# Masked graph attention on one core: the stores of h on ScalarE's queue, the stores of u on SyncE's, and an eleventh warming matmul

## The chip, the cores and the metric

The kernel runs on one core of a Trainium2 chip. Its engines are TensorE (PE in the profile, PEld for its weight loads), VectorE (DVE), ScalarE (ACT), GpSimd (POOL) and SyncE (SP), which only issues DMAs. ScalarE and GpSimd can issue DMAs too. The metric is the device time of one execution in microseconds; a time for a kernel is the median of its runs.

## The reference

A layer of attention over a sparse graph with 2708 nodes and 1024 features, after a layer norm, with a residual:

```python
h = jnp.maximum(_layernorm(x, axis=-1), 0.0)
q = h @ W_q.T + b_q;  k = h @ W_k.T + b_k;  v = h @ W_v.T + b_v
z = (q @ k.T) / sqrt(1024)
z = z * adj                                   # adj: 0 or 1, about 4 ones in a row
z = jnp.where(z == 0.0, -10000.0, z)
out = x + relu(softmax(z, axis=1) @ v)
```

## The kernel before

The kernel never forms the 2708 x 2708 scores. It finds the few neighbours of each node in the adjacency, sorts the nodes by their number of neighbours, and works on 22 row tiles of 128 nodes (the last has 20). Three streams run beside each other.

The matmul stream is TensorE's. After `WARM` matmuls on zeros (lines 497 and 498), which depend on nothing but a cleared tile, it forms M from W_q and W_k in a fast scheme of blocks (line 463: `term`, in PSUM banks ps_x, ps_y, ps_z; ScalarE takes the results out in `evicted`, line 477, VectorE in `joined`). Then come 20 units, each two row tiles against one matrix of 1024 x 1024 in a block scheme of seven products (`multiply`, line 982, matmuls at line 948). Ten units are "q" (rows of h times M) and ten are "o" (rows of u times W_v); one tile is left alone at the end. Before a unit its rows are transposed (`half_turned`, line 402, tiles pt) and copied out by ScalarE (`held`, line 684). ScalarE also sets the starting value of two banks (`banks_for`, line 713), copies a bank to psy and to p5 (lines 961 and 964), and copies results.

The preparing stream loads x (line 218) and the adjacency (line 347) on SP, forms h in place on ScalarE (`apply`, line 263), counts ones on ScalarE (`counted`, line 355) and finds their places on VectorE (line 376). The factors r of the layer norm come from GpSimd (`root`, lines 246 to 254). Each tile of h is written to DRAM (`keep`, line 270) and summed into `hsum` on GpSimd (lines 272 and 285). A tile's buffer is used again for a later tile of x, and that load waits for both the store and the sum. The table of neighbours is scattered to DRAM in sorted order by GpSimd (`put`, line 613) in two parts, late tiles first, and read back (`reload`, line 625); the part of tiles 0 to 7 is the early table.

The attention stream gathers rows of h by the table on GpSimd (line 597), forms scores on VectorE (line 826) against q, which SP loads (line 799), and weighted sums u on VectorE (line 879), whose first term is ScalarE's (line 871). Ten of the u tiles are written to `u_dram` (`sums`, line 888) and read back by SP as rows of an "o" unit (line 1142, tiles or); the other tiles stay in SBUF. SP also stores q (line 1022), stores combinations of W_v in `tv_dram` (line 768) and reloads M and T for the "o" units (line 1247).

The order on ScalarE and VectorE is the order of the code through the first four units, and on VectorE through all of the units; GpSimd's is written by hand up to the table's reload. The string `steps_at` and the calls of `follow` place single steps (h and k are `keep`, a is `apply`, p is `counted`, r is `root`) between the products. A planner orders the rest, SP among it. Each engine works through its own instructions strictly in that order.

Of the kernel before, what the change touches and what calls it, by code (L numbers as in the profile page):

```python
# [18 lines left out]
P = 128  # L19
# [10 lines left out]
EARLY = 8  # L30
# [4 lines left out]
WIDE = 8  # L35
MOMENTS = (0, 1, 2, 3, 6, 7)
ROOT = 32
WARM = 10
SEARCH = tuple(range(EARLY, 22)) + tuple(range(EARLY))
BATCHES = ((0, 3), (4, 7), (8, 11), (12, 12), (13, 13), (14, 17), (18, 21))  # L40
MLIMIT = 61.0 / 512
# [22 lines left out]
def tile_preln_masked_attention(  # L64
# [12 lines left out]
    nc = tc.nc  # L77
# [23 lines left out]
    h_dram = dram.tile([N, D], FT, name="h_dram")  # L101
    q_dram = dram.tile([EARLY * P, D], FT, name="q_dram")
    q_late = dram.tile([(BARE - EARLY) * P, D], FT, name="q_late")
    u_dram = dram.tile([FULL * P, D], FT, name="u_dram")
# [30 lines left out]
    ptab = tab  # L135
# [30 lines left out]
    t = 0  # L166
    while t < NT:
# [4 lines left out]
        t = e  # L172
# [92 lines left out]
    def keep(first, add=True):  # L265

        group, xs, r = normed.pop(first)
        for t, xt in zip(group, xs):
            t0, n = tiles[t]
            (nc.scalar if 6 <= t <= 10 else nc.gpsimd).dma_start(h_dram[t0:t0 + n, :], xt[:n])  # L270
            if add:
                nc.gpsimd.tensor_add(hsum[:n], hsum[:n], xt[:n])
            else:
                owed[t] = xt
# [21 lines left out]
    def follow(steps):  # L296

        for step in steps.split():
# [11 lines left out]
            elif step[0] in "hk":  # L310
                keep(first, step[0] == "h")
            elif step[0] == "+":
                owe(first)
            elif step[0] == "p":
                counted(first)
            elif step[0] == "c":
                counts(*halves[first])
            elif step[0] == "o":
                sorted_at.append(sort(*halves[first]))
            elif step[0] == "w":  # L320
                pooled.close()
                with tc.issue_after((behind if first < EARLY else products)[-1].ins):
                    entered.append(put(first, int(last[0]) + 1))
            elif step == "z":
                pooled.enter_context(tc.manual_schedule(engines={mybir.EngineType.Pool}))
                with tc.issue_after(entered[-1].ins):
                    reload(EARLY, NT)
            elif step[0] == "b":
                reload(*halves[first])
            elif step[0] == "g":  # L330
                squared(first)
            else:
                if step[0] == "e":
                    counted(first)
                if step[0] != "j":
                    found(first, *[range(int(o[0]), int(o[-1]) + 1) for o in only])
                if step[0] != "i":
                    listed(first)
# [94 lines left out]
    with tc.tile_pool(name="w", bufs=1, side="left") as wp:  # L433
# [62 lines left out]
        zeros = hsum.bitcast(BF)  # L496
        for i in range(WARM):
            cleared = nc.tensor.matmul(Y[i % H], zeros[:, :P], zeros[:, :NB], start=True, stop=True)  # L498
# [122 lines left out]
    def reload(lo, hi):  # L621

        full = min(hi, FULL)
        src = tab_dram[lo >= EARLY]
        loads = [nc.gpsimd.dma_start(ptab[:, lo:full, :], src[:(full - lo) * P, :].rearrange("(t p) w -> p t w", p=P))]
        if hi > FULL:
            loads.append(nc.gpsimd.dma_start(ptab[:REST, FULL, :], src[(FULL - lo) * P:, :]))
        for load in loads:
            for put in puts[lo >= EARLY]:
                tc.add_manual_dep(load.ins, put.ins.name,  # L630
                                  mybir.DependencyInfo(mybir.DependencyClass.Sync, mybir.DependencyReason.DATA),
                                  reason="every row of the part")
        return loads[-1]
# [171 lines left out]
    def fill():  # L805
        while wanted and free:
            t, s = wanted.pop(0)
            g = free.pop(0)
            with tc.issue_after(first_q[0].ins) if first_q else nullcontext():
                gathered.append(gather(g, h_dram[:, :], t, s, P, skip=True))  # L810
            g_of[t].append(g)

    def chained(step):

        with tc.issue_after(chain[-1].ins):
            chain.append(step())
# [58 lines left out]
    def sums(t):  # L875
        u, coef = us.pop(t)
        for s in range(0 if t in EMPTY else 1, K[t]):
            fill()
            chained(lambda: nc.vector.scalar_tensor_tensor(  # L879
                u, g_of[t][s], coef[:, at[t][s]:at[t][s] + 1], u, op0=ALU.mult, op1=ALU.add))  # L880
            free.append(g_of[t][s])
            yield 1.3
        fill()
        g_of.pop(t)
        if near(t):
            held[t] = u
        else:
            nc.gpsimd.dma_start(u_dram[t * P:(t + 1) * P, :], u)
        done.add(t)

    def marked(lo, hi):
# [5 lines left out]
    def attention(order):  # L897
        for t in order[:2]:
            ask(t)

        fetch(order[0])
        fill()
        yield 0.0
        marked(0, EARLY)
        free.extend(slots[:8])
        fill()
        yield 0.0
        after = order[1:] + [None, None]
        yield from scores(order[0], after[0])
        for i, t in enumerate(order):  # L910
            nxt = after[i]
            ahead = nxt is not None and K[t] + K[nxt] <= HIGH + 1
            part = scores(nxt, after[i + 1]) if nxt is not None else iter(())
            if ahead:

                for _ in range(min(2, K[nxt] - 1)):
                    yield next(part, 0.0)
            weights(t)
            yield 0.6
            if ahead:  # L920
                yield from part
            yield from sums(t)
            yield from part
# [9 lines left out]
    def near(t):  # L933

        return t == alone or any(t in unit[1:] for unit in units[:now[0] + 3] if unit[0] == "o")
# [72 lines left out]
    lo, hi = slice(0, NB), slice(NB, D)  # L1008
# [295 lines left out]
    with tc.If(some > 0):  # L1304
# [19 lines left out]
        with tc.tile_pool(name="big", bufs=1, side="right") as big, tc.tile_pool(  # L1324
# [34 lines left out]
            with tc.For_i(0, NT) as i:  # L1359
# [35 lines left out]
                for b0 in range(0, N, NB):  # L1395
                    w = min(NB, N - b0)
# [23 lines left out]
                u = gen.tile([P, D + 1], FT, tag="q", name="g_uu")  # L1420
# [60 lines left out]
```

## Time and profile before

| | |
|---|---|
| time, median of 3 runs | 646.41 us (645.72, 646.41, 652.27) |
| profiled execution, its own time | 645.97 us |
| span from first to last instruction | 644.2 us |
| mean granted TensorE clock | 0.997 |
| busy PE / DVE / ACT / POOL | 635.7 / 524.4 / 279.8 / 399.2 us |
| DMA queues, share of 16 engines | POOL's 46.7%, SP's 35.0%, ScalarE's 2.4% |

In the views an engine's name with a q (ACTq, SPq) is its sequencer, which issues DMAs and waits. A row of a timeline has the start and the length in us, engine, line, operation, output<-input and, in brackets, how long the engine sat idle before it and what ended that. A row of a group by source line has the shortest, median and longest duration in ns, and the first and last start in us.

### The profile page before, as it was taken

To read this page: it belongs to the slowest core of one execution; us is meant where nothing else is said; L and a number is where in the kernel's file an instruction comes from. 1 tells how busy PE (TensorE), PEld (TensorE's weight loads), DVE (VectorE), ACT (ScalarE), POOL (GpSimd) and SP (SyncE) were. 2 spreads that over 40 slices of the span, in tenths; PEclk is the share of its full clock that TensorE was granted. 3 is DMA by queue.
4 is the path that set the end of the run, shared out by engine and by line. 5 is a ranking of instruction groups with operands and counts; after the bars stand their busy time and mean duration, and the time that the engine had idled before them with its cause. 6 is when DMAs were issued, how large, how long until landed. Compare 5 with 4: busy or idle time off the path is not lost.

```text
span 644.2 us, 6376 instructions
## 1 busy us (share of the span) xinstructions
PE 635.7 (99%) x1730; PEld 326.2 (51%) x1730; DVE 524.4 (81%) x1014; ACT 279.8 (43%) x426; POOL 399.2 (62%) x428
## 2 busy tenths in 40 slices
PE   9999999999999999999999999999999999999995
PEld 5777766444444444545444444444444544444442
DVE  5999599998896755998988969987999999988121
ACT  3539877958586622413223134332433434423200
POOL 2649991885868457765845536655785868781431
PEclk9999999999999999999999999999999999999998
DMA  8993999599789969997978999988798989895741
GB/s 342 407 362 139 385 342 387 214 323 359 239 313 355 381 206 397 348 356 259 332 248 294 419 415 311 285 269 258 231 338 270 285 303 324 252 285 122 174 135 70
DMA packets 61012, 189.02 MB, mean 293 GB/s; under 512 B 9711, under 2 KB 10047, under 8 KB 60074
## 3 DMA queue, kind: packets, MB, share of 16 engines
q0 software_dynamic: 31728, 98.74, 46.7%
q1 hardware_dynamic: 27514, 84.04, 35.0%
q10 hardware_dynamic: 1728, 5.77, 2.4%
q8 instruction: 16, 0.26, 0.2%
q14 instruction: 26, 0.21, 0.1%
HBM read 159.81 MB, written 42.31 MB: 314 GB/s over the span
## 4 chain that ended last, share of the span: by engine, by line
PE 98%; ACT 0%; POOL 0%; DVE 0%; POOLq 0%; issue 0%
PE ps L948 45%; PE psy L948 32%; PE ps_y L463 6%; PE pt L402 5%; PE ps_x L463 4%; PE ps_z L463 4%; PE ps_y L498 1%; PE ps_h L1153 0%; PE ps_v L581 0%; ACT a L684 0%; DVE y_alone L1297 0%; POOL out_dram L1281 0%; ACT M L477 0%; POOLq L1303 0%; ACT ps L713 0%
## 5 line engine op out<-in xcount | busy, mean ns | idle before, releaser
L597 POOL DMA_INDIRECT g<-h_dram,tab x105 | 127.5, 1214 | 61.3 <-issue 23.5
L948 PE MATMUL ps<-M,a 128*128 128x512 f32 x320 | 144.0, 593 | 0.1
L948 PE MATMUL psy<-wlow,s 128*128 128x512 f32 x320 | 143.9, 592 | 0.0
L826 DVE SCALAR_TENSOR_TENSOR junk<-g,pq 128x1024 uint8<-128x1024 f32 x93 | 113.8, 1223 | 8.1 <-DMA g<-h_dram,tab 6.3
L879 DVE SCALAR_TENSOR_TENSOR u<-g,coef,u 128x1024 f32<-128x1024 f32 x79 | 101.3, 1283 | 5.6 <-ACT u L871 3.7
L948 PEld LDWEIGHTS ps<-M,a 128*128 128x128 f32 x320 | 59.4, 190 | 68.2 <-issue 67.7
L948 PEld LDWEIGHTS psy<-wlow,s 128*128 128x128 f32 x320 | 59.2, 190 | 67.0 <-issue 66.2
L376 DVE FIND_INDEX8 at<-ones,adj 128x8 uint32<-128x685 f32 (+1 forms) x88 | 74.5, 865 | 0.0
L948 PE MATMUL psy<-wlow,a 128*128 128x512 f32 x160 | 72.2, 592 | 0.0
L948 PE MATMUL ps<-wlow,s 128*128 128x512 f32 x160 | 72.0, 593 | 0.0
L948 PE MATMUL ps<-M,s 128*128 128x512 f32 x160 | 71.9, 592 | 0.0
L355 ACT ACTIVATE sized<-adj 128x2708 uint8<-128x2708 f32 (+1 forms) x22 | 54.3, 2468 | 14.2 <-DMA adj<-in_adj_dram 13.4
L1047 POOL DMA_INDIRECT y<-in_x_dram,tab x19 | 34.1, 1793 | 30.6 <-DMA tail_dram<-y 12.5
L285 POOL TENSOR_TENSOR hsum<-hsum,x 128x256 f32<-128x256 f32 (+1 forms) x56 | 38.7, 729 | 22.3 <-DVE wlow L431 15.6
L948 PEld LDWEIGHTS ps<-wlow,s 128*128 128x128 f32 x160 | 30.3, 190 | 38.5 <-issue 36.8
L948 PEld LDWEIGHTS psy<-wlow,a 128*128 128x128 f32 x160 | 30.3, 190 | 37.8 <-issue 37.3
L948 PEld LDWEIGHTS ps<-M,s 128*128 128x128 f32 x160 | 30.3, 190 | 37.8 <-issue 37.3
L778 POOL DMA_INDIRECT out_dram<-y,tab x21 | 29.2, 1392 | 17.3 <-DMA y<-in_x_dram,tab 9.9
L684 ACT COPY a<-pt 128x512 f32<-128x512 f32 x60 | 33.3, 589 | 2.4 <-PE psy L948 2.4
L597 POOL DMA_INDIRECT M<-h_dram,tab x20 | 25.7, 1287 | 13.1 <-ACT u L871 4.6
L688 DVE TENSOR_TENSOR s<-a,pt 128x512 f32<-128x512 f32 x40 | 25.6, 680 | 6.7 <-ACT a L684 5.5
L871 ACT ACTIVATE u<-g,coef 128x1024 f32<-128x1024 f32 x16 | 18.4, 1149 | 25.9 <-DVE coef L870 21.0
(240 smaller groups left out, 867.8 us busy)
## 6 DMA issues: line engine op xcount, KB each, us to landing
adj<-in_adj_dram SPq DMA_DIRECT2D x21, 1354.0 KB
x<-in_x_dram SPq DMA_DIRECT2D x21, 512.0 KB
h_dram<-x POOLq DMA_DIRECT2D x16, 512.0 KB
q_late<-q SPq DMA_DIRECT2D x12, 512.0 KB
pq<-q_late SPq DMA_DIRECT2D x12, 512.0 KB
u_dram<-u POOLq DMA_DIRECT2D x10, 512.0 KB
or<-u_dram SPq DMA_DIRECT2D x10, 512.0 KB
g<-in_wv_dram SPq DMA_DIRECT2D x16, 256.0 KB
```

Of the source, the lines that this page charges most:

```text
L285: small.append(nc.gpsimd.tensor_add(hsum[:n, cols], hsum[:n, cols], xt[:n, cols]))
L355: nc.scalar.activation(sized[:n], a[:n, :, :PW], AF.Abs, accum_out=total[:n, t:t + 1])
L376: nc.vector.max_index(at[:n, k - first_k, g, :], ones[:n, 0:8], a[:n, g, :])
L402: nc.tensor.transpose(pt[:, c, :], xt[:, k * P:(k + 1) * P], ident)
L463: mm = nc.tensor.matmul(bank, a_tile(o + H * a[0], a[1], i), b(o), start=first and o == 0, stop=(o == H - 1), skip_group_check=True)
L597: return nc.gpsimd.indirect_dma_start(out=dst, out_offset=None, in_=src, in_offset=off, bounds_check=N - 1, oob_is_err=False)
L684: nc.scalar.copy(ops[name], bank)
L778: to = nc.gpsimd.indirect_dma_start(out=out, out_offset=bass.IndirectOffsetOnAxis(ap=ptab.bitcast(U32)[:n, t, SLOTS:SLOTS + 1], axis=0), i ...
L826: chained(lambda: nc.vector.scalar_tensor_tensor(junk, g_of[t][s], 1.0, tq[t], op0=ALU.mult, op1=ALU.mult, accum_out=zall[:, t, s:s + 1]))
L879: chained(lambda: nc.vector.scalar_tensor_tensor(u, g_of[t][s], coef[:, at[t][s]:at[t][s] + 1], u, op0=ALU.mult, op1=ALU.add))
L948: mm = nc.tensor.matmul(bank, a[:, c, :], b[:, c, :], start=False, stop=(c == 3), skip_group_check=True)
L1047: return nc.gpsimd.indirect_dma_start(out=y[:n], out_offset=None, in_=x, in_offset=off, compute_op=ALU.add)
```

## The change

The stores of h of all tiles are issued by ScalarE, where before it issued those of tiles 6 to 10 and GpSimd the others; their place in ScalarE's order is the place of the `keep` step. The stores of u and the reload of the early table are issued by SP instead of GpSimd. One more warming matmul is issued.

```diff
-WARM = 10
+WARM = 11
@@ def keep(first, add=True):
-            (nc.scalar if 6 <= t <= 10 else nc.gpsimd).dma_start(h_dram[t0:t0 + n, :], xt[:n])
+            nc.scalar.dma_start(h_dram[t0:t0 + n, :], xt[:n])
@@ def reload(lo, hi):
-        loads = [nc.gpsimd.dma_start(ptab[:, lo:full, :], src[:(full - lo) * P, :].rearrange("(t p) w -> p t w", p=P))]
+        loads = [(nc.gpsimd if lo >= EARLY else nc.sync).dma_start(ptab[:, lo:full, :], src[:(full - lo) * P, :].rearrange("(t p) w -> p t w", p=P))]
@@ def sums(t):
-            nc.gpsimd.dma_start(u_dram[t * P:(t + 1) * P, :], u)
+            nc.sync.dma_start(u_dram[t * P:(t + 1) * P, :], u)
```

## The prediction

> **What bounds the kernel now.** I read the head of the page and its chain first, then busy time by stretches, then the chain in order of time.
>
> ```profile
> span 644.2 us, 6376 instructions
> PE 635.7 (99%) x1730; PEld 326.2 (51%) x1730; DVE 524.4 (81%) x1014; ACT 279.8 (43%) x426; POOL 399.2 (62%) x428
> PE 98%; ACT 0%; POOL 0%; DVE 0%; POOLq 0%; issue 0%
> ```
>
> TensorE is busy for 635.7 of 644.2 us and 98% of the chain that ended last is its own. Only 8.5 us of the span are without it. The next view says where they are: its columns are the stretch, its length, then busy time and count for each engine.
>
> ```profile
> 34.00:104.00 70.00, 70.00 (x168) 50.59 (x167) 62.55 (x141) 50.62 (x59) 52.17 (x78) 1.00 0.83 310
> 107.00:340.00 233.00, 233.00 (x649) 110.41 (x649) 194.30 (x418) 115.41 (x167) 155.36 (x192) 1.00 0.86 310
> 340.00:637.00 297.00, 297.00 (x819) 140.53 (x817) 238.45 (x383) 95.57 (x170) 174.55 (x133) 1.00 0.83 272
> ```
>
> In three stretches that make up 600 us TensorE is busy for the whole of each, at the full granted clock (1.00). The matmuls' ends are modelled, so a wait of a tenth of a microsecond could hide here, a wait of one could not. What is left are the start, the end, and a seam near 104 us, seen in the chain (start, length, what):
>
> ```profile
> 1.19 4.17 PE ps_y L498 x10
> 5.37 0.07 issue
> 5.44 27.83 PE ps_x L463 x64
> ...
> 103.69 0.60 ACT M L477
> ...
> 105.74 0.50 ACT ps L713
> 106.25 0.04 issue
> 106.29 7.13 PE ps L948 x16
> 113.42 3.43 PE psy L948 x8
> ...
> 120.29 0.22 PE pt L402 x2
> ...
> 135.12 3.43 PE psy L948 x8
> ...
> 626.65 10.42 PE ps L948 x24
> ...
> 638.35 0.69 POOL out_dram L1281
> ```
>
> The start is 1.19 us of clearing, 4.17 us of warming matmuls, and then products without a break. At 103.69 the chain passes through ScalarE to 106.25, while TensorE does transposes. The products end at 626.65 + 10.42 = 637.07, and the last 7 us are VectorE, one scatter and its landing. None of the moved DMAs is in this chain. So the change can hardly gain; the question is whether it makes TensorE wait.
>
> **The eleventh warming matmul (line 498).** It comes before the first product, and this one cannot start until its first weight has landed.
>
> ```profile
> L498 PE MATMUL ps_y<-hsum x10: 380/631/631, 1.2 to 5.0; 128*128 128x512 bf16 x10
> 4.99 0.38 PE L498 MATMUL ps_y<-hsum 128*128 128x512 bf16 x1
> 5.33 1.06 ACT L492 ACTIVATE junk_w<-wlow 128x1024 uint8<-128x1024 f32 x1 [1.83 <-DMA wlow<-in_wq_dram]
> ```
>
> The ten start from 1.19 to 4.99, 3.80 / 9 = 0.42 us apart; the last is shorter than the others (0.38 against 0.63 us), so the array has sped up by then. The weight landed at 5.33 (ScalarE's first square waits for the same tile) and the product began at 5.44. From below the eleventh costs nothing, filling the time from the tenth's start to 5.44; from above it costs a whole step, 0.42 us. The tenth is its nearest row, and an eleventh like it would start before 5.4 and run on a little past 5.44: I take +0.2 us, and keep 0 and 0.42.
>
> The Trainium skill, "TensorE: Matmul & The Clock Gate", section "Part 1: The HAM clock gate", says that the array runs at half clock for a time of about 3.4 us and not for a number of matmuls, in a window that runs freely and so differs between runs. The trace agrees as far as it goes: the change of pace comes at the tenth, 3.8 us after the first start. By this rule ten at 0.42 us already cover the window in this execution, and the eleventh would be pure cost; in a run where the window falls later it would cost the full step, and the sum would be 0.2 us higher.
>
> One transpose of tile 2 also changes place: before, six of the eight run ahead of the first product of the main loop and two at 120.29 (0.22 us); after, seven run ahead, where TensorE waits for ScalarE's copy until 106.25 anyway, and one is left. That takes 0.11 us off the path.
>
> **Stores of h to ScalarE (line 270).** 17 stores leave POOL, five are on ScalarE already and give the price.
>
> ```profile
> L270 POOL DMA_DIRECT2D h_dram<-x x17: 531/558/658, 56.8 to 137.1; - x17
> L270 ACTq DMA_DIRECT2D h_dram<-x x5: 338/344/348, 152.6 to 184.1; - x5
> 152.60 1.48 ACTq L270 DMA_DIRECT2D h_dram<-x  x2
> 154.17 0.59 ACT L1026 COPY q<-ps 128x512 f32<-128x512 f32 x1 [0.47 <-ACT x L263]
> ```
>
> POOL gives back 17 x 0.558 = 9.5 us. ScalarE takes 0.34 us for each, and the copy behind the pair starts at 154.17, after the pair ends at 154.08, 0.47 us after the last compute: 0.45 us per store, 7.7 us in all. ScalarE's order is written by hand and stands unchanged; the stores enter in batches of 4, 4, 5, 2 and 2, behind evictions, counts and copies that the trace shows at about 54.7, 73, 90.5, 106.7 and 130.6. What follows each batch on ScalarE, and what it waits for today:
>
> ```profile
> 60.77 0.60 ACT L477 ACTIVATE M<-ps_y 128x512 f32<-128x512 f32 x1 [1.50 <-PE ps_y L463]
> 78.50 2.47 ACT L355 ACTIVATE sized<-adj 128x2708 uint8<-128x2708 f32 x1 [1.72 <-DMA adj<-in_adj_dram]
> 94.63 2.37 ACT L263 ACTIVATE x<-x,r 128x1024 f32<-128x1024 f32 x2 [4.08 <-POOL r L253]
> 103.69 0.60 ACT L477 ACTIVATE M<-ps_y 128x512 f32<-128x512 f32 x1 [1.82 <-PE ps_y L463]
> 110.03 0.57 ACT L961 COPY psy<-ps 128x512 f32<-128x512 f32 x1 [0.75 <-PE ps L948]
> 131.72 0.57 ACT L961 COPY psy<-ps 128x512 f32<-128x512 f32 x1 [1.16 <-PE ps L948]
> ```
>
> Batch one, 1.8 us, meets 1.50 us of waiting for TensorE, batch two, 1.8 us, meets 1.72 us, batch three, 2.25 us, meets 4.08 us; what is left over, 0.4 us, fits in the 1.82 us ahead of 103.69. These waits may shrink, since r comes from POOL, which is then earlier by eight stores (4.5 us), but a wait that shrinks brings ScalarE forward by as much. Batch four, 0.9 us, meets 0.75 us: the copy into psy ends about 0.15 us later than 110.60, and the product that reads it starts at 113.42. Batch five, 0.9 us, fits in 1.16. On the path: 0, with cover to spare of 1.4 us at 103.69 and 2.6 us at 113.42. If that cover were gone, each store would cost its 0.45 us.
>
> A store also waits: its tile (made on ScalarE itself), and a completion counter. In the built program the hardware DMAs of SP and ScalarE take eight counters in turn, and a DMA is issued only when the eighth before it has landed. Going through all 17, each such DMA is issued well before ScalarE reaches the store, the closest being loads of x or adjacency issued some ten microseconds ahead. I take 0.
>
> On SP the loads of x and adjacency also change places, since the stores' counters and an earlier POOL shift them: one adjacency load goes ahead of x_1, which had been held by a store and a sum; another goes behind x_5. Both feed VectorE and ScalarE work with microseconds to spare; 0 on the path.
>
> **Stores of u and the early table to SP (lines 888, 625).**
>
> ```profile
> L888 POOL DMA_DIRECT2D u_dram<-u x10: 571/578/602, 264.6 to 550.4; - x10
> 232.60 0.95 POOL L625 DMA_DIRECT2D tab<-tab_dram  x1 [2.51 <-DMA tab_dram<-tab,pos_i]
> ```
>
> POOL gives back 10 x 0.578 + 0.95 = 6.7 us and the waits in front of them. SP does no compute, but a store that waits for VectorE's last sum holds every load behind it. I compared each u's last sum with SP's next DMA of today. The two closest:
>
> ```profile
> 303.22 1.28 DVE L879 SCALAR_TENSOR_TENSOR u<-g,coef,u 128x1024 f32<-128x1024 f32 x1
> 306.77 0.32 SPq L1022 DMA_DIRECT2D q_late<-q  x1
> 538.36 2.60 DVE L879 SCALAR_TENSOR_TENSOR u<-g,coef,u 128x1024 f32<-128x1024 f32 x2
> 538.46 16.68 SPq L1142 DMA_DIRECT2D or<-u_dram  x3
> 553.33 1.04 PE L402 MATMUL pt<-ident,or 128*128 128x128 f32 x8
> ```
>
> u_3 ends at 304.50 and SP's next DMA starts at 306.77: 2.3 us to spare. Only one store stands ahead of a load that was earlier: u_18, ready at 540.96, is now ahead of the load of row tile 20, issued at 538.46 before. That load slips by about 3 us; its rows are transposed at 553.33, nearly 15 us after today's issue. The table waits for POOL's eight scatters wherever it is issued (232.60); behind it on SP stand a store of q that is read last of all, and stores for which VectorE's subtractions are awaited anyway. 0 on the path.
>
> **Sum.** +0.2 - 0.1 = +0.1 us on the profiled execution of 645.97 us (644.2 span): 646.1. The median of the runs before is 646.41, 0.44 above that execution; half of this distance added gives **646.3 us**. A measurement of this kernel tells about 1% (6.5 us) from no change.
>
> **Rivals.**
> First, slower: the issue itself blocks ScalarE. SP shows that it can:
>
> ```profile
> 29.96 5.34 SPq L218 DMA_DIRECT2D x<-in_x_dram  x1
> ```
>
> This one load took 5.34 us to issue behind two adjacency loads, where a store takes 0.34. If a store in batch three, four and five met the same (5.0 us extra each), the cover would leave 5.0 - 3.65 = 1.4 us at 103.69 (4.08 + 1.82 - 2.25 = 3.65), 5.0 - 2.6 = 2.4 us at 113.42, and 2.1 us at 135.12 (copy of 131.72 ending at 137.2): 5.9 us, 652.3; one of them alone gives about 648.5. It decides from 2.6 us of extra issue time in batch four. Against it: ScalarE's own five issues, beside adjacency loads as well, lie within 338 to 348 ns. Chance 0.09, a third of it beyond 1%.
>
> Second, SP held by u: if VectorE is late with u_18 by more than the 9 us or so that remain after a load, the transposes of 553.33 wait; 15 us late would give 646.3 + 6 = 652. Against it: VectorE gets its gathers from a POOL with 16 us less to do. Chance 0.04.
>
> Third, the window of the clock falls later and the eleventh costs 0.42 us: 646.5. Chance 0.12; inside my range.
>
> Fourth, the lighter POOL shows as a gain. It would need TensorE time that isn't there between 5.44 and 637.07; only the 7 us behind the last product remain, and their scatter (638.35) waits for VectorE, not for earlier DMAs. One microsecond at most: 645.3. Chance 0.03.
>
> **How the numbers follow.** Forecast 0.72. Low end 645.2, the fourth rival; high end 649.0, one blocked batch. Faster by over 1% 0.02, within 1% 0.92, slower 0.06 (a third of the first rival, most of the second, and 0.01 for what I don't see).
>
> **What would show it.** Right: TensorE busy about 636 us; 11 matmuls at line 498 and the first product at 5.4 to 5.9; L270 22 times on ACTq at 0.34 to 0.5 us; POOL about 16 us less busy; the first ps product of line 948 at 106.3 to 106.8. Wrong: an L270 issue of microseconds on ACTq, a TensorE gap at 104 to 136 released by ACT, or a gap near 553 released by the load of or.

## The result, and the profile after

The changed kernel takes 645.7 us (median of 21 runs, 644.62 to 649.39) against 649.58 us for the kernel before, run beside it (21 runs, 645.72 to 652.78). The ratio is 0.9954, with a 95% interval of 0.9936 to 0.9971: 0.3% to 0.6% faster. The runs of before were 3 us slower than the three that the prediction started from. In a second comparison, with the full change again (e5_all below), before took 646.54 and the change 645.46, ratio 0.9976 (0.9962 to 0.999). So the gain is small, real, and depends on how slow before is just then. The prediction was 646.3 with no change that can be told. Three later executions of before, at 675 us and more, ran at a granted clock of 0.946 or less and are left out of every ratio and count.

The profiled execution took 646.32 us. The page's span, busy times and chain:

```profile
span 644.5 us, 6383 instructions
...
PE 636.8 (99%) x1731; PEld 326.5 (51%) x1731; DVE 521.3 (81%) x1014; ACT 279.8 (43%) x426; POOL 376.3 (58%) x400
...
PE 94%; DVE 3%; DMA 2%; issue 0%; POOL 0%; POOLq 0%; SPq 0%
```

By its span this execution is 0.3 us longer than that of before. A reader who stops here sees "nothing happened"; the chain says otherwise: it was 98% PE before, and now 3% of it is VectorE's and 2% a DMA's. The view of TensorE's waits names the places (line waited for, us in total, times, longest), and the chain in order of time gives the ends:

```profile
PE ps_y L498 <- POOL hsum L112: 1.2, 1, 1.2
PE ps L948 <- DVE s L688: 0.8, 1, 0.8
PE ps L948 <- ACT ps L713: 0.6, 1, 0.6
```
```profile
1.19 4.88 PE ps_y L498 x11
...
107.11 7.08 PE ps L948 x16
...
628.92 10.42 PE ps L948 x24
...
640.61 0.69 POOL out_dram L1281
```

Before had only the first of those three waits. The products now end at 628.92 + 10.42 = 639.34, 2.3 us later than the 637.07 of before. Of these, 0.8 us were lost ahead of the first product of the main loop (107.11, against 106.29 before), and 1.4 us are the two new waits. And yet the span is only 0.3 us longer: behind the last product 1.9 us have gone. Effects of opposite sign, which the prediction's sum did not have, almost cancel in this execution.

**The tail.** Timeline rows of the last scatter, and the rows of the closing instructions grouped by source line (shortest, median, longest in ns, first and last start). Before:

```profile
638.07 0.96 POOL L1281 DMA_INDIRECT out_dram<-y_alone,half_i  x1 [1.68 <-DVE y_alone L1297]
```
```profile
L1477 POOLq DRAIN  x3: 46/115/4720, 638.6 to 643.9; - x3
L1477 SPq DRAIN  x3: 7/7/13, 641.7 to 643.6; - x3
```

After:

```profile
640.33 0.97 POOL L1281 DMA_INDIRECT out_dram<-y_alone,half_i  x1 [1.67 <-DVE y_alone L1297]
```
```profile
L1477 POOLq DRAIN  x3: 46/109/2697, 640.9 to 644.3; - x3
L1477 SPq DRAIN  x3: 7/7/13, 643.6 to 643.9; - x3
```

GpSimd's last act is a drain. It took 4.72 us before and 2.70 us after. From the scatter's start to the end of the span there were 644.2 - 638.07 = 6.1 us, and are 644.5 - 640.33 = 4.2. These rows are no "busy" work, so the head of the page and the chain don't count them.

**The search.** SP's timeline, VectorE's at the same place, and VectorE's waits for the adjacency. Before:

```profile
45.31 15.28 SPq L218 DMA_DIRECT2D x<-in_x_dram  x4
60.69 0.55 SPq L347 DMA_DIRECT2D adj<-in_adj_dram  x1
```
```profile
70.83 0.09 DVE L376 MATCH_VALUE_LOAD at<-ones,adj 128x8 f32 x1 [6.52 <-DMA adj<-in_adj_dram]
```
```profile
DVE at L376 <- DMA adj<-in_adj_dram: 12.6, 4, 6.5
```

After:

```profile
46.09 2.48 SPq L218 DMA_DIRECT2D x<-in_x_dram  x3
48.67 0.55 SPq L347 DMA_DIRECT2D adj<-in_adj_dram  x1
```
```profile
64.05 0.03 DVE L376 MATCH_VALUE_LOAD at<-ones,adj 128x8 f32 x1
```
```profile
DVE at L376 <- DMA adj<-in_adj_dram: 10.0, 7, 2.5
DVE at L376 <- issue: 5.3, 1, 5.3
```

Before, SP's fourth load of x, at 60.27, stands ahead of the adjacency load; its buffer becomes free with GpSimd's store of h, first issued at 56.8. VectorE idles 6.5 us for that adjacency and then works to about 150 us with hardly a gap. After, the adjacency load goes out 12 us sooner and the long wait at 70 us is gone; up to 150 us the waits that are left are of 2.5 us and less. One of 5.3 us comes later, at 178.40. The view puts it down to `issue`, but the chain in order of time comes to it through an adjacency load (166.43 to 176.57), and goes on from it, over the search's last steps, to the subtraction at line 688 for which TensorE waits 0.8 us. Before, VectorE idled 3.1 us at the same place (176.13), and TensorE did not wait.

**The ScalarE side** is as harmless as forecast where the stores stand:

```profile
L270 ACTq DMA_DIRECT2D h_dram<-x x22: 338/350/802, 51.3 to 185.5; - x22
```
```profile
69.06 1.15 ACT L234 ACTIVATE junk_x<-x,mv 128x1024 uint8<-128x1024 f32 x1
69.07 1.39 ACTq L270 DMA_DIRECT2D h_dram<-x  x3
```

The second fence shows three stores being issued while one activation runs.

### The profile page after: what moved, and what is told of

Its sections match the earlier page's. It is cut to its first block, busy times and chain, and to the rows that moved or that the text cites. A ratio compares the mean times of both kernels' runs of the same rounds, so it can differ in the third digit from the quotient of the medians.

```text
span 644.5 us, 6383 instructions
## 1 busy us (share of the span) xinstructions
PE 636.8 (99%) x1731; PEld 326.5 (51%) x1731; DVE 521.3 (81%) x1014; ACT 279.8 (43%) x426; POOL 376.3 (58%) x400
## 4 chain that ended last, share of the span: by engine, by line
PE 94%; DVE 3%; DMA 2%; issue 0%; POOL 0%; POOLq 0%; SPq 0%
PE ps L948 42%; PE psy L948 30%; PE ps_y L463 6%; PE pt L402 5%; PE ps_x L463 4%; PE ps_z L463 4%; DMA adj<-in_adj_dram 2%; DVE at L376 1%; PE ps_y L498 1%; DVE st L224 1%; PE ps_h L1153 0%; PE ps_v L581 0%; DVE cand L394 0%; DVE sort L668 0%; DVE y_alone L1297 0%
## 5 line engine op out<-in xcount | busy, mean ns | idle before, releaser
L597 POOL DMA_INDIRECT g<-h_dram,tab x105 | 124.4, 1184 | 70.4 <-issue 22.0
L1047 POOL DMA_INDIRECT y<-in_x_dram,tab x19 | 32.8, 1726 | 32.5 <-ACT taken L1013 11.2
L778 POOL DMA_INDIRECT out_dram<-y,tab x21 | 27.8, 1323 | 17.5 <-DMA y<-in_x_dram,tab 9.2
```

The lines of the kernel that those rows point to most:

```text
L597: return nc.gpsimd.indirect_dma_start(out=dst, out_offset=None, in_=src, in_offset=off, bounds_check=N - 1, oob_is_err=False)
L778: to = nc.gpsimd.indirect_dma_start(out=out, out_offset=bass.IndirectOffsetOnAxis(ap=ptab.bitcast(U32)[:n, t, SLOTS:SLOTS + 1], axis=0), i ...
L1047: return nc.gpsimd.indirect_dma_start(out=y[:n], out_offset=None, in_=x, in_offset=off, compute_op=ALU.add)
```

## The experiments

Twelve kernels, in three groups. The times of before beside them were 646.55, 646.54 and 647.39 us.

### One part at a time

The four parts of the diff, each alone, on the kernel before:

```diff
e1_warm  +WARM = 11
e2_h     +nc.scalar.dma_start(h_dram[t0:t0 + n, :], xt[:n])            # all tiles
e3_u     +nc.sync.dma_start(u_dram[t * P:(t + 1) * P, :], u)
e4_tab   +(nc.gpsimd if lo >= EARLY else nc.sync).dma_start(ptab[:, lo:full, :], ...)
```

> Only the eleventh warming matmul. The theory of the search stage (the gain comes from the stores of h, because loads of x and adjacency and the factors r come earlier and TensorE is spared waits between 100 and 200 us in some executions) expects no gain: ratio to before 1.000 to 1.001. The theory of the clock (ten warming matmuls do not always keep the array busy until the first product, and it then stays slow longer) expects this run to hold the whole gain: ratio about 0.995 and the spread of the runs gone. The theory of the attention stage expects 1.000.

> Only the stores of h on ScalarE, ten warming matmuls. The theory of the search stage expects the whole gain here: ratio about 0.995, most executions at 645 to 647 us. The theories of the clock and of the attention stage expect 1.000, with the wide spread of before (645.7 to 652.8).

> Only the stores of u on SP. The theory of the attention stage (GpSimd, 6 us lighter and no longer held at a store until VectorE is done, gathers earlier, and products after 230 us wait less) expects about 0.995. The theories of the search stage and of the clock expect 1.000.

> Only the load of the early table on SP. All three theories expect 1.000, within the noise of a comparison of five rounds; it moves one issue of 0.95 us that waits for the scatters of the table wherever it stands.

| | median us | ratio (95%) | drain, us | scatter to end, us |
|---|---|---|---|---|
| e1_warm | 646.31 | 0.9999 (0.9986 to 1.0013) | 4.73 | 6.1 |
| e2_h | 646.06 | 0.9988 (0.9973 to 1.0004) | 3.46 | 4.8 |
| e3_u | 647.08 | 1.0004 (0.999 to 1.0018) | 3.95 | 5.3 |
| e4_tab | 646.08 | 0.9996 (0.998 to 1.0011) | 4.11 | 5.5 |

By time alone, no part differs from before, so none of the three theories in these expectations, each of which had the whole gain of 0.995 in one part, came out. The traces tell more than the times: each of the three moves shortens the drain, the eleventh matmul doesn't. And only the h part has TensorE waiting after the start, here in e2_h:

```profile
PE ps L948 <- DVE s L688: 0.8, 1, 0.8
PE ps L948 <- ACT ps L713: 0.3, 1, 0.3
```

Going back from that wait leads to ScalarE's two stores of q at line 1022. Before:

```profile
138.59 1.11 ACTq L1022 DMA_DIRECT2D q_dram<-q  x2
139.75 1.06 ACT L233 ACTIVATE junk_x<-x 128x1024 uint8<-128x1024 f32 x1 [0.58 <-ACT q L1037]
```

In e2_h:

```profile
138.81 2.23 ACTq L1022 DMA_DIRECT2D q_dram<-q  x2
141.08 1.06 ACT L233 ACTIVATE junk_x<-x 128x1024 uint8<-128x1024 f32 x1 [1.69 <-DMA x<-in_x_dram]
```

In the built program the DMAs of SP and ScalarE take eight counters in turn, so that each waits until the eighth before it, of either engine, has landed. The second q store shares its counter with the load of row tile 7 in before. Two h stores (tiles 4 and 5) now stand between that load and the store, so in e2_h it shares it with the load of row tile 8, issued later. ScalarE stands still behind it for 1.1 us more, its copies at line 713 come late, and TensorE has to wait for them near 156 us.

### The whole change again, and three theories

Now the theories were: the tail and this rotation of the eight counters; an early chain in which some executions of before lose 2 us; and a result that belonged to its chip.

```diff
e5_all      the change
e6_ut       the change in u and the table only
e7_keep45   the change, and:
-            nc.scalar.dma_start(h_dram[t0:t0 + n, :], xt[:n])
+            (nc.gpsimd if t in (4, 5) else nc.scalar).dma_start(h_dram[t0:t0 + n, :], xt[:n])
e8_again    the kernel before
```

> The whole change again, beside the kernel before on one chip. Theory of the tail and the rotation: the closing drain of GpSimd shrinks with the transfers taken off its queue (last scatter's start to the end of the span 4.2 us, 6.1 before), and two h stores more between the load of row tile 7 and the second q store make that store wait for a later load, so TensorE idles 1.2 to 1.5 us near 156 and 184 us; ratio 0.997 to 0.999. Theory of the early chain (with h on GpSimd some executions lose 2 us and more before 120 us): few times above 647.5 here, many before; ratio 0.995 to 0.998. If the result's 0.9954 belonged to its chip alone: 0.998 to 1.0005.

> The stores of u and the load of the early table on SyncE, h stores and warming as before. Tail and rotation: no wait of TensorE after 100 us, the tail shortened by 0.77 plus 0.62 us to about 4.7 us, span 642.6 to 643.2, ratio 0.9975 to 0.999. Early chain: as many executions late by 2 us as the kernel before has, so its median follows theirs, 0.998 to 1.0005.

> The whole change, but the h stores of row tiles 4 and 5 stay on GpSimd, so that the second q store again waits for the load of row tile 7. Tail and rotation: the waits near 156 and 184 us are gone (under 0.2 us together), tail 4.2 us as with the whole change, span about 643.1, ratio 0.002 below that of the whole change. Rival (the stores themselves take ScalarE's time there): both waits stay at 1.2 to 1.5 us and the time is that of the whole change.

> The kernel before once more, for another of its executions. Early chain: if this one comes out above 647.5 us, TensorE idles 2 us or more between 60 and 120 us, released by VectorE or by an adjacency load; if it comes out at 646, there is no wait. Clock theory: a late execution has the same waits, but the clock opens later than 4.95 us. Tail: last scatter's start to the end 6.1 us in either.

| | median us | range | ratio (95%) |
|---|---|---|---|
| e5_all | 645.46 | 643.85 to 647.33 | 0.9976 (0.9962 to 0.999) |
| e6_ut | 646.69 | 645.0 to 647.73 | 0.9994 (0.9982 to 1.0005) |
| e7_keep45 | 643.98 | 643.81 to 644.79 | 0.9956 (0.994 to 0.9972) |
| e8_again | 646.57 | one run | |

e7_keep45 is the clearest of the study. Two stores are put back, and neither wait is there:

```profile
138.71 1.09 ACTq L1022 DMA_DIRECT2D q_dram<-q  x2
```
```profile
PE ps_y L498 <- POOL hsum L112: 1.2, 1, 1.2
PE ps_x L463 <- DMA wlow<-in_wq_dram: 0.6, 1, 0.6
```

The q stores take 1.09 us again, TensorE waits for nothing after the start, and the median is 1.5 us below the whole change beside it (0.2% of 645 us is 1.3, as expected). It is faster than both kernels. The rival, that the stores' own time causes the waits, falls: 15 of the 17 are still there.

For the wait at line 713 the cause is shown: it is in the three profiles that have all stores of h on ScalarE (the change, e2_h, e5_all) and in no other. Its price is less sure than the median says. The two profiled executions, e5_all and e7_keep45, differ by 1.6 us (spans 643.8 and 642.2); 0.7 of it is that wait, and another 0.7 is an earlier first product of the main loop (106.51 against 107.19), which two stores issued after 127 us do not explain.

e5_all showed the wait at line 713 (0.7 us) and not the other, less than the 1.2 to 1.5 expected: the second, near 185 us, hangs on an adjacency load's landing and isn't in every execution. Nor does it need the two stores: e11_ten below, which has them on GpSimd like e7_keep45, shows it in part.

```profile
PE ps L948 <- DVE s L688: 0.4, 1, 0.4
```

e8_again came out at 646.57 us, with 6.1 us from the last scatter to the end and no wait of 2 us, so it says nothing of late executions. e6_ut closed in 4.8 us, as expected, but its ratio is 0.9994 and not the 0.9975 to 0.999 of the tail alone. It was caught in a late execution (647.47 us), among whose waits is this one:

```profile
PE pt L402 <- ACT M L477: 1.0, 2, 0.8
```

It leads back to GpSimd making the factors of tiles 2 and 3. The same three operations before:

```profile
93.80 0.20 POOL L251 TENSOR_TENSOR r<-r 128x2 f32<-128x2 f32 x1
94.08 0.23 POOL L252 TENSOR_SCALAR r<-mv 128x2 f32<-128x2 f32 x1
94.40 0.20 POOL L253 TENSOR_TENSOR r<-r 128x2 f32<-128x2 f32 x1
```

In e6_ut, with the group of VectorE's subtractions at line 431 (the "sums" of the expectations) in a second fence:

```profile
93.77 2.27 POOL L251 TENSOR_TENSOR r<-r 128x2 f32<-128x2 f32 x1
96.12 1.28 POOL L252 TENSOR_SCALAR r<-mv 128x2 f32<-128x2 f32 x1
97.48 1.02 POOL L253 TENSOR_TENSOR r<-r 128x2 f32<-128x2 f32 x1
```
```profile
L431 DVE TENSOR_TENSOR wlow<-M x4: 1217/1219/1228, 93.6 to 115.3; 128x1024 f32<-128x1024 f32 x4
```

The subtractions began at 95.0 in the profile of before, just behind GpSimd's chain, and at 93.6 here, in the middle of it: operations of 0.2 us took 1.0 to 2.3.

### The collision, ten matmuls, and the drain by itself

```diff
e9_h15    -(nc.scalar if 6 <= t <= 10 else nc.gpsimd).dma_start(h_dram...)
          +(nc.scalar if 6 <= t <= 10 or 15 <= t <= 18 else nc.gpsimd).dma_start(h_dram...)
e10_late  +eng = nc.gpsimd; [eng.memset(r, 0.0) for _ in range(5 if first == 2 else 0)]
e11_ten   e7_keep45 with WARM = 10
e12_split -nc.gpsimd.dma_start(u_dram[t * P:(t + 1) * P, :], u)
          +[nc.gpsimd.dma_start(u_dram[t * P:(t + 1) * P, c:c + NB], u[:, c:c + NB]) for c in (0, NB)]
```

> As before, but the four h stores of row tiles 15 to 18 on ScalarE; nothing else. Theory of the collision: GpSimd then makes the scales of row tiles 2 and 3 (lines 246 to 254) some 2 us sooner, ending near 92.8 us, ahead of VectorE's long sums at line 431 (from 93.6 at the earliest), so none of its small operations takes over 0.8 us and few executions come out above 647.2 (1 in 3 before); with 0.3 us less of tail the median is 645.5 to 646.0, ratio 0.998 to 0.9995. Rival (late executions come from the clock or from loads): as many late ones as before, ratio 0.9995 to 1.0005.

> As before, but GpSimd clears the tile of the scales five times ahead of making those of row tiles 2 and 3 (about 1.4 us). Theory of the collision: the last of lines 246 to 254 run while VectorE's sums at line 431 do and take 1.0 to 2.5 us each in place of 0.2, the scales come 3 to 4 us later, TensorE idles 0.8 to 2.5 us between 103 and 113 us, and nearly all executions are above 647; ratio 1.001 to 1.004. Rival (the 1.4 us are hidden, no collision): the small operations stay at 0.2 us, 0.9995 to 1.0005.

> The change with the h stores of row tiles 4 and 5 left on GpSimd, and ten warming matmuls in place of eleven. Theory: no wait of TensorE after the start, tail 4.2 us, 643.6 to 644.3; against 643.98 with eleven it differs by under 0.5 us, as the matmul's 0.43 us is covered in part by the wait for the first weights. If the eleventh helps by bringing the clock up sooner: 644.5 to 645.5.

> As before, but each store of u on GpSimd in two halves of its columns: the same bytes, twice the pieces. Tail by pieces: the closing drain grows by as much as taking the u stores away shortened it, 0.76 us, from 4.72 to about 5.5 us, and the last scatter's start to the end of the span from 6.1 to 6.9. Tail by bytes: 4.72 and 6.1 as before. Its time may also move in the middle, which is not what it is for.

**The collision is real and does not set the time.** In e10_late, where the five clears took 0.8 us and not 1.4, lines 253 and 254 took 2.19 and 1.27 us under VectorE's subtractions, as expected. But TensorE did not wait near 103 us, and the median is 647.17 (ratio 1.0011, 0.9991 to 1.003): ScalarE could use the factors from 97.4 us on, against 98.5 in e6_ut, and that much was still hidden. e9_h15 was to take the collision away by making the factors 2 us sooner. They did not come sooner (the last ends at 95.0, as in before at 94.9), but its profiled execution is a late one (647.96 us) and its operations stay at 0.2 us: an execution can be late without a collision. Nor is the kernel faster: 647.62 us, ratio 1.001 (0.9993 to 1.0027), 7 of 12 runs above 647.2. So the collision is not what the late executions have in common. What e9_h15 leaves as it was is the hold on SP:

```profile
60.67 0.55 SPq L347 DMA_DIRECT2D adj<-in_adj_dram  x1
```
```profile
70.70 0.09 DVE L376 MATCH_VALUE_LOAD at<-ones,adj 128x8 f32 x1 [6.43 <-DMA adj<-in_adj_dram]
```
```profile
PE ps_in L662 <- DVE sort L650: 0.8, 1, 0.8
```

The stores of tiles 11 to 14, not 15 to 18, hold SP until 60; VectorE idles its 6.4 us, then idles again for a later adjacency load (from 79.7 to 82.2), and TensorE waits 0.8 us for its sort near 152 us. The profile of before has the first idle time and not the second, and no such wait. Sorting all runs by this one feature: of the kernels whose stores of tiles 11 to 14 are on GpSimd (before, e1, e3, e4, e6, e9, e10) 73 of 168 runs are above 647.2 us, of those where they are on ScalarE (the change, e2, e5, e7, e11) 5 of 54. But the bound was chosen after the fact, and the five kernels also close 1.3 to 1.9 us sooner, which alone takes runs below it. With the bound lowered for each kernel by what its traced closing is shorter, the counts are 82 of 168 and 30 of 54; at 1.6 us above each kernel's own fastest run, 74 of 168 and 18 of 54. So the count does not show that the hold makes executions late.

**The drain grows with the rows sent by plain DMAs from GpSimd's queue.** e12_split (one execution) doubles the pieces of the u stores and leaves their bytes:

```profile
L1477 POOLq DRAIN  x3: 46/115/5542, 638.4 to 644.5; - x3
```

5.54 us, where 5.5 was expected by pieces and 4.72 by bytes. With pieces of 128 rows as the unit, the kernels with one part moved or added agree: 16.2 units of h off the queue -1.26 us, 10 of u -0.77, the table's 8 (one DMA of 1024 rows) -0.61, four of h (e9_h15, 4.44) -0.28, ten more in e12_split +0.82. That is 0.07 to 0.08 us a unit, whenever in the kernel they were sent; the table, one DMA, rules out a count of DMAs. Moved together they save less: the whole change would so come to 4.72 - 34.2 x 0.077 = 2.1 us, and has 2.70. Nor is 2.70 a plain lower limit, since e7_keep45, with two units of h back on the queue, has 0.18 us more:

```profile
L1477 POOLq DRAIN  x3: 46/115/2872, 638.5 to 641.9; - x3
```

Why the parts together save 2.0 us and not 2.6 is not shown.

e11_ten: 644.23 us, ratio 0.9963 (0.9951 to 0.9976), against 0.9956 (0.994 to 0.9972) with eleven. The two stand in different groups of runs; the eleventh matmul can't be told from none, alone (e1_warm) or here.

## Why the prediction was right, and where it was not

The time, 645.7, lies in the range of 645.2 to 649.0 and within 1% of before. The sum behind it was not right. It gave +0.1 us for the profiled pair, and what the profiles show is -1.9 (the closing), +1.4 (the two waits) and +0.8 (the start), three terms that were at nothing or too small and nearly cancel. So that the time fits is in part luck. So is its base: the sum started from 646.41, and the median of before came out at 649.58.

*"Only the 7 us behind the last product remain, and their scatter (638.35) waits for VectorE, not for earlier DMAs. One microsecond at most."* This step of the fourth rival failed. The scatter does wait for VectorE, but what follows it was taken as given; it holds a drain of 4.72 us that shrinks with the transfers moved, worth 1.9 us in span. Each moved part has its share, by e2_h, e3_u and e4_tab.

*"Going through all 17, each such DMA is issued well before ScalarE reaches the store ... I take 0."* The stores themselves don't wait long (0.80 us at most, median 0.35). The step failed because it looked at the moved DMAs only: a DMA inserted in a rotation of eight changes the wait of every DMA in the next eight, here of a q store that was already on ScalarE. By e7_keep45 the two stores cost the wait at line 713, 0.6 and 0.7 us in the two profiles of the whole change; the medians put the difference at 1.5 us.

*"One adjacency load goes ahead of x_1 ... microseconds to spare; 0 on the path."* The move was seen; what it is worth stays open. In the profiled execution of before TensorE lost no time to the search. One profile can't show the executions where it does, and the first three runs, 646.41, 645.72 and 652.27, were a hint of them. That the freed load makes fewer runs late is not shown: e9_h15 is one trace, the count of runs doesn't settle it, and a kernel with nothing but that load moved was not run. Why the adjacency lands late in one execution and not in another stays open, as does the 649.58 of before in the first comparison, and with it most of the gain measured there.

*ScalarE's 0.45 us a store, 7.7 us in all against waits of 0.75 to 4.08.* The conclusion, 0 on the path, held for the batches; the price was too high, since it took the last pair, which is issued between computations, for all. Stores are issued while an activation runs, as the fence above shows. The first rival (an issue of 5 us on ScalarE) did not come: 0.80 us was the longest, though that is beyond the 0.34 to 0.5 named as a sign of being right.

*The eleventh matmul, +0.2 (0 to 0.42).* In the profiled pair it cost the upper bound, and a little more:

```profile
4.15 1.91 PE L498 MATMUL ps_y<-hsum 128*128 128x512 bf16 x4
5.86 1.57 PE L463 MATMUL ps_x<-wlow 128*128 128x512 f32 x2
```

The first product began at 5.86, not 5.44, and two products took 1.57 us where later ones start 0.43 apart: the array was still at half pace. The third rival (the window falls later) is what this execution shows, with 0.35 us on top (the third product at 7.27, against 6.50 before), and the first product of the main loop came at 107.11, outside the 106.3 to 106.8 that was named. In e1_warm's profile the first product began at 5.86 too and the next ones kept the pace of before; its span is 0.4 us longer than that of before. In e7_keep45 it was faster from the ninth matmul on, three in 0.81 us:

```profile
4.22 0.81 PE L498 MATMUL ps_y<-hsum 128*128 128x512 bf16 x3
```

So the window does move from run to run, by more than one matmul covers. The Trainium skill, "TensorE: Matmul & The Clock Gate", section "Part 1: The HAM clock gate", says that the window runs freely; the traces agree.

*GpSimd about 16 us less busy.* It was 399.2 - 376.3 = 22.9; the moved DMAs are 16.2 of it. Most of the rest is in the indirect transfers, which took GpSimd a little less time each: the 105 gathers at line 597 into g took 1214 ns each before and 1184 after, 3.1 us in all. Why is not shown.

*u and the table on SP, 0 on the path.* Held: nothing of e3_u's or e4_tab's waits is released by a load on SP after the start, and the second rival's wait near 553 us is absent.

## What to carry to other kernels

When a DMA is moved to another queue, look at the next eight that share its counters, on either queue, as well as at the DMA itself: it may be someone else's transfer that starts to wait. Read the rows behind the last useful instruction, which no busy time counts, and keep plain stores off GpSimd's queue if the end of the kernel waits for its drain. And one profile shows one execution: where runs of one kernel lie 3 us and more apart, their spread is part of the evidence, and a bound for "late" has to move with whatever else a kernel saves.

## What was not expected of the hardware

GpSimd's closing drain took 2.69 to 5.54 us over the kernels here. Each 128 rows that its queue had sent by plain DMAs, at any time before, were worth 0.07 to 0.08 us where one part was moved, and 0.06 on average over the whole change.

GpSimd's operations on 128 x 2 values took 0.2 us alone and 1.0 to 2.3 us while VectorE subtracted two tiles of 128 x 1024 in SBUF (1.22 us for each operation). The Trainium skill, "SBUF — State Buffer", section "SBUF: two separate sides", says that a VectorE operation with two SBUF inputs and a GpSimd operation that reads SBUF lock a port pair against each other for a whole instruction rather than share it. The trace agrees: line 251 in e6_ut, started 0.14 us behind the first subtraction, ended at 96.04, when the second had ended (95.98), and no sooner.
